# A message-passing kernel: GpSimd's gathers in the order in which they are written, with other waits

## The chip, the core and the metric

The kernel runs on one core of one Trainium2 chip. The metric is the device time of one execution in microseconds (us). Engines are named as in the profile: PE (TensorE, its weight loads in a row of their own, PEld), DVE (VectorE), ACT (ScalarE), POOL (GpSimd), SP (SyncE, which only issues DMAs here). L281 is line 281 of the kernel.

## The reference

It is one layer of a graph network with 6250 nodes of 128 features, and 100,000 edges that are sorted by their destination.

```python
msg_in = concat([x[src], x[dst], edge_attr], axis=1)      # 100000 x (128 + 128 + 4)
h = silu(msg_in @ mW1 + mb1)
messages = h @ mW2 + mb2
aggregated = segment_sum(messages, dst, num_segments=6250)
u = silu(concat([x, aggregated], axis=1) @ uW1 + ub1)
y = layer_norm(x + u @ uW2 + ub2)                          # ln_g, ln_b
out = layernorm(x + y)
```

All of it is float32.

## The kernel before, in words

The edges are cut into 98 groups of 1024 edges (8 tiles of 128 edges; the last group has 6 tiles). The part of the first layer that belongs to the source node is computed once for each node: `tab_a` = x @ mW1[:128], and so is the part of the destination, `tab_b`. Both tables are written to DRAM. For each group the source part is then fetched row by row: `fetch(g)` starts 8 indirect DMAs on POOL, each of which gathers 128 rows of 128 floats into one eighth of a buffer `ga`. There are six such buffers, so group g + 6 takes over the buffer of group g. Groups 0 to 4 (`g < RAW`) gather rows of x itself, since the table isn't there yet; PE multiplies these by the weights later, which is why they are turned first (`turn_rows`, `turn_late`).

The tables are made in 7 parts of 8 node tiles (`for k, (i0, n) in enumerate(parts)`): PE transposes x (L343), ACT copies it (L344), PE multiplies (L386), ACT copies one half of the products (L388) for `tab_a` and DVE adds a bias to the other (L389) for `tab_b`, and SP starts the two writes (L392, L393). They use three tiles of psum in turn. Between these parts stand the lists of destinations (`destination_lists`, k = 2) and the turning of the groups 0 to 3 (L365 on PE, L366 on DVE).

The loop over groups then does at step g, for later groups as well:

- `load(g + 4)` on SP: 96 rows of `tab_b` into `mv`, edge attributes into `st`
- `hidden(g)`: DVE adds the gathered rows to the products (`s`, L635), ACT makes silu of it (`h`, L636); for g < 5 ACT alone
- `products(g + 2)`: 8 matmuls of PE (L619), for g < 5 with 8 more of the gathered rows (L622)
- `node_matrix(g + 3)` and `edge_matrix(g + 1)` on DVE: matrices of zeros and ones (L592, L605)
- `by_nodes(g)`: 8 matmuls of PE (L647) that sum the edges of a node; DVE adds the sums of group g - 2 to `acc` (L660)
- `fetch` of a group further on
- one step of a `node_batch`, the second layer for some 512 nodes (L510 to L560)

A matmul on float32 appears as two rows of PE and two of PEld in the profile, a transpose as one of each. At g = 4 `destination_checks` and at g = 5 `fuse_weights` are inserted, both with short exchanges between PE and DVE or ACT.

The order of the instructions of SP, PE, DVE and ACT is the order in which they are written (`manual_schedule`). POOL is not in that list: its instructions are ordered by the framework's scheduler. In the program as built, this scheduler issues of a group gathers 1, 2, 3, 5, 6, 7 ahead of those gathers which have a wait added by hand; in the steady part gather 0 of group g comes 8th, and gather 4 follows behind the first three of group g + 1.

Waits are added by hand in `fetch(g, *after)` with `add_manual_dep`: with two instructions in `after`, gather 0 waits for the first and gather 4 for the second. `begun[g]` is the first matmul of `products(g)`, `summing[g]` the first of `by_nodes(g)`. From group 14 on (`CLOSE`) group g + 2 is fetched at step g and waits for `begun[g + 2]` and `summing[g]`. Groups 8 to 13 are fetched at every second step, and wait for `begun` of two groups. Besides these, the first gather of a group that is issued waits until the buffer is free, and each gather waits for the landing of the eighth before it.

Of the kernel before, what the change touches and what calls it, by code (L numbers as in the profile page):

```python
# [14 lines left out]
ENG = mybir.EngineType  # L15
# [9 lines left out]
def kernel(  # L25
# [40 lines left out]
    nc = tc.nc  # L66
# [13 lines left out]
    CLOSE = 14  # L80
    LEAD = 4
    RAW = 5
# [14 lines left out]
    def groups(n, g):  # L97
        return [(i, min(g, n - i)) for i in range(0, n, g)]
# [12 lines left out]
    batches.append((NT - LAST, LAST, NG))  # L111

    edges = ExitStack()
    edges.enter_context(tc.manual_schedule(engines={ENG.SP, ENG.PE, ENG.DVE, ENG.Activation}))
    gath = edges.enter_context(tc.tile_pool(name="gath", bufs=6))
    work = edges.enter_context(tc.tile_pool(name="edge", bufs=2))

# [4 lines left out]
    def wide():  # L122
        return tables_ps.tile([P, G, P], F32, name="wide")
# [50 lines left out]
    ident = consts.tile([P, P], F32, name="ident")  # L174
# [48 lines left out]
    def destination_lists():  # L223
        base_c = work.tile([NG, 1], F32, name="base_c", bufs=1)
        nc.vector.tensor_copy(base_c, dst_l[:, 0:1])
        rel_n = work.tile([P, GE], F32, name="s")[:NG]
        nc.vector.tensor_scalar(rel_n, dst_l, base_c, None, op0=OP.subtract)

        near_n = work.tile([P, GE], F32, name="s")[:NG]
        nc.vector.tensor_scalar(near_n, rel_n, float(W), -1.0, op0=OP.min, op1=OP.max)  # L230
        near_u = tpool.tile([NG, GE], U8, name="near_u")
        nc.vector.tensor_scalar(near_u, near_n, 1.0, None, op0=OP.add)
        nc.sync.dma_start(near_d[:, :], near_u)
        by_lane(rel, rel_n)
        row = to_row(base_c, NG)
        nc.vector.tensor_copy(base_f, row)
        nc.vector.tensor_copy(base_i, row)
# [34 lines left out]
    rows, bases, near = {}, {}, {}  # L272

    def tiles_of(g):
        return min(G, -(-(E - g * GE) // P))

    def fetch(g, *after):

        rows[g] = gath.tile([P, G, H], F32, name="ga")
        for i in range(tiles_of(g)):  # L280
            ins = nc.gpsimd.indirect_dma_start(  # L281
                out=rows[g][:, i, :],
                out_offset=None,
                in_=x if g < RAW else tab_a[:, :],
                in_offset=bass.IndirectOffsetOnAxis(
                    ap=src_i[:, g, i : i + 1] if g else src_0[:, i : i + 1], axis=0
                ),
            )
            part, at = divmod(i * len(after), G)
            if after and at == 0:  # L290
                tc.add_manual_dep(
                    ins.ins,
                    after[part].ins.name,
                    mybir.DependencyInfo(
                        mybir.DependencyClass.Sync, mybir.DependencyReason.DATA
                    ),
                    reason="TensorE keeps up with the gathers",
                )
# [8 lines left out]
    def attributes(c):  # L307
        t = turn.tile([EQ, EJ * ED], F32, name="ea_l")
        chunk = edge_attr[c * EC : (c + 1) * EC]
        nc.sync.dma_start(t, chunk.rearrange("(q j) d -> q (j d)", q=EQ))  # L310
        ea_l[c] = t
# [21 lines left out]
    def by_node(t):  # L333
        return t[:NP].rearrange("(i p) f -> p i f", p=P)
# [5 lines left out]
    def turn_x(i0, n):  # L340
        pt = wide()
        for i in range(n):
            ins = nc.tensor.transpose(pt[:, i, :], x_sb[:, i0 + i, :], ident)  # L343
        nc.scalar.copy(xT[:, i0 * P : (i0 + n) * P], pt[:, :n, :].rearrange("p i f -> p (i f)"))  # L344
        return ins
# [12 lines left out]
    parts = groups(NT, G)  # L358
    table = []

    def turn_rows(g):

        px = wide()
        for i in range(G):
            nc.tensor.transpose(px[:, i, :], rows[g][:, i, :], ident)  # L365
        nc.vector.tensor_copy(rows[g], px)  # L366

    def turn_late(g):
        for lo in range(0, G, BT):
            px = node_y()  # L370
            for i in range(BT):
                nc.tensor.transpose(px[:, i, :], rows[g][:, lo + i, :], ident)
            nc.vector.tensor_copy(rows[g][:, lo : lo + BT], px)

    fetch(1, turn_x(*parts[0]))
    for k, (i0, n) in enumerate(parts):
        if k + 1 < len(parts):
            turn_x(*parts[k + 1])

        tb = x_sb[:, i0 : i0 + n, :]  # L380
        ta = tpool.tile([P, G, H], F32, name="t", bufs=2)
        for j0, m in groups(n, G // 2):
            pm = wide().rearrange("p (i s) f -> p i s f", s=2)
            for j in range(m):
                cols = slice((i0 + j0 + j) * P, (i0 + j0 + j + 1) * P)
                ins = nc.tensor.matmul(pm[:, j], xT[:, cols], w1, start=True, stop=True)  # L386
            own = slice(j0, j0 + m)
            nc.scalar.copy(ta[:, own], pm[:, :m, 0, :])  # L388
            nc.vector.tensor_add(  # L389
                tb[:, own], pm[:, :m, 1, :], b1[:, None, :].to_broadcast([P, m, H])  # L390
            )
        nc.sync.dma_start(by_node(tab_a)[:, i0 : i0 + n, :], ta[:, :n])  # L392
        nc.sync.dma_start(by_node(tab_b)[:, i0 : i0 + n, :], tb)  # L393
        table.append(ins)
        if k == 0:
            attributes(0)
        if k == 1:
            fetch(2, *table)
            for t in mv:
                nc.sync.dma_start(t[W:], mW1[2 * H :])  # L400
        if k == 2:
            destination_lists()
        if k == 3:
            fetch(3, *table[2:])
            attribute_rows(0)
            turn_rows(0)
        cols = slice(i0 * P, NW if i0 + n == NT else (i0 + n) * P)
        nc.vector.memset(acc[:, cols], 0.0)
        if k == 4:
            fetch(4, table[4])  # L410
            destinations(0)
            load_bases(0)
            turn_rows(1)
    for g in range(2, TURNED):
        turn_rows(g)
    if E < NG * GE:
        pad = tpool.tile([ED, NG * GE - E], F32, name="pad")
        nc.vector.memset(pad, 0.0)
# [5 lines left out]
    def rows_ps():  # L424
        return ps.tile([P, G, P], F32, name="pre")

    def node_y():
        return node_ps.tile([P, BT, H], F32, name="y")
# [181 lines left out]
        )  # L610
        return oh

    begun, summing = {}, {}

    def products(g):
        pre = rows_ps()
        st = stbuf[g % NST].rearrange("k (i c) -> k i c", i=G)
        for i in range(tiles_of(g)):
            ins = nc.tensor.matmul(pre[:, i, :], st[:, i, :], mv[g % NM], start=True, stop=g >= RAW)  # L619
            begun.setdefault(g, ins)  # L620
            if g < RAW:
                nc.tensor.matmul(  # L622
                    pre[:, i, :], rows[g][:, i, :], w1[:, 0, :], start=False, stop=True
                )
        return pre

    def hidden(g):
# [24 lines left out]
    def by_nodes(g, h, oh):  # L652

        pt = degrees(g)
        sums(g, pt, h, oh, 0, tiles_of(g))
        return pt
# [14 lines left out]
    oh, h, pt, running = {0: edge_matrix(0)}, {}, {}, []  # L671
    pre = {g: products(g) for g in range(2)}

    for g in range(RAW, 8):
        fetch(g)
    for g in range(NG):
        if g == 3:
            load_weights()
        if g == 4:
            destination_checks(node_y())  # L680
        if g == 5:
            fuse_weights()
        for c in range(1, NC):
            if g == max(1, c * EC // GE - 10):
                attributes(c)
            if g == max(1, c * EC // GE - 10) + 1:
                attribute_rows(c)
        if g + LEAD < NG:
            load(g + LEAD)
        last = g >= NG - 1  # L690
        if not last:
            h[g] = hidden(g)
        if TURNED <= g + 2 < RAW:
            turn_late(g + 2)
        if g + 2 < NG:
            pre[g + 2] = products(g + 2)
        if g + MADE < NG:
            node_matrix(g + MADE)
        if g + 1 < NG:
            oh[g + 1] = edge_matrix(g + 1)  # L700
        if g - 2 in pt:
            add(g - 2, pt.pop(g - 2))
        if last:
            break
        pt[g] = by_nodes(g, h.pop(g), oh.pop(g))
        if CLOSE <= g + 2 < NG:
            fetch(g + 2, begun[g + 2], summing[g])
        elif g % 2:
            at = g // 2 + 8
            fetch(at, begun[g + 1], begun[g + 2])  # L710
        if g >= NG - 3:
            add(g - 1, pt.pop(g - 1))
        for i0, n, first in batches[:-1]:
            if g == (first if first >= NG - 3 else first + 1):
                running.append(node_batch(i0, n, *node_tiles(nodes, node_y)))
        for _ in range(2 if g >= NG - 6 else 1):
            advance(running)

    g = NG - 1
# [194 lines left out]
```

## Time and profile before

| | us |
|---|---|
| median of 3 runs (1204.91 to 1206.64) | 1206.59 |
| the profiled execution, its own time | 1194.18 |
| its span, first to last instruction | 1192.3 |
| POOL busy, 790 instructions | 740.9 |
| PE busy, 3655 rows | 723.3 |
| DVE busy | 488.3 |
| ACT busy | 244.9 |

The mean granted clock of PE was 0.685 of full speed. The span is that of one profiled execution, and the durations of single instructions come from it. A row of POOL named DMA_INDIRECT is one gather of 128 rows. The bracket behind a row of the timeline is the time for which the engine had been idle, and what ended it; "issue" means that the profile shows no wait, and "remote" that the one who ended it is not known to it.

### The profile page before, as it was taken

What the parts mean: (1) busy time and instruction counts of PE and PEld (TensorE: products, weight loads), DVE (VectorE), ACT (ScalarE), POOL (GpSimd) and SP (SyncE); (2) the same over time, 40 slices, a digit from 0 to 9 for tenths busy, and PEclk for the clock granted to TensorE, in tenths of its full rate; (3) what the DMA queues carried; (4) which work ended last, traced back from release to release, by engine and by line L of the source; (5) the groups of instructions that cost most, each with busy time, mean ns of one, the idle gap of its engine ahead of it and who ended that gap; (6) DMA issues with size and microseconds to landing.
All of it is one profiled execution on the core that took longest, in us unless ns stands there. A gap on an engine that the chain in (4) does not pass through costs nothing.

```text
span 1192.3 us, 11417 instructions
## 1 busy us (share of the span) xinstructions
PE 723.3 (61%) x3655; PEld 646.4 (54%) x3655; DVE 488.3 (41%) x1023; ACT 244.9 (21%) x306; POOL 740.9 (62%) x790
## 2 busy tenths in 40 slices
PE   3765388655755664575466466566556575565664
PEld 3655378545655654465465456456556464555553
DVE  3460366352443343334335325225326335236253
ACT  1221024112112222212122103102202202112233
POOL 7536456766666666566566666666666666666650
PEclk9787667766765676667667667666676666676765
DMA  7653123223222222232222223213322222222210
GB/s 187 177 164 89 37 60 83 71 53 79 77 64 66 79 69 65 54 91 60 76 71 64 73 52 85 73 49 78 83 51 79 79 52 75 74 53 64 57 48 24
DMA packets 70222, 88.96 MB, mean 75 GB/s; under 512 B 20720, under 2 KB 51839, under 8 KB 70155
## 3 DMA queue, kind: packets, MB, share of 16 engines
q0 software_dynamic: 25024, 51.30, 17.5%
q1 hardware_dynamic: 40552, 34.96, 9.9%
q10 hardware_dynamic: 4578, 1.89, 0.7%
q8 instruction: 31, 0.51, 0.2%
q14 instruction: 37, 0.30, 0.1%
HBM read 76.71 MB, written 11.38 MB: 74 GB/s over the span
## 4 chain that ended last, share of the span: by engine, by line
issue 39%; POOL 25%; PE 16%; another core or an unknown queue 6%; DVE 5%; DMA 1%; DVEq 1%; ACT 1%; SPq 0%; POOLq 0%; ACTq 0%
POOL ga L281 25%; PE pre L619 7%; PE pt L647 6%; DVEq L635 1%; DVE oh L605 1%; DMA ga<-tab_a,src_i 1%; DVE s L635 1%; DVE st L484 1%; PE y L526 1%; DVE y L528 1%; PE y L517 0%; PE y L510 0%; PE y L511 0%; PE y L512 0%
## 5 line engine op out<-in xcount | busy, mean ns | idle before, releaser
L281 POOL DMA_INDIRECT ga<-tab_a,src_i x742 | 701.8, 946 | 393.7 <-issue 194.4
L619 PE MATMUL pre<-mv,st 100*128 100x128 f32 x1564 | 315.7, 364 | 195.8 <-issue 141.7
L647 PE MATMUL pt<-oh,h 128*128 128x96 f32 x1564 | 292.2, 341 | 188.5 <-issue 177.5
L619 PEld LDWEIGHTS pre<-mv,st 100*128 100x128 f32 x1564 | 286.3, 271 | 215.6 <-issue 168.1
L647 PEld LDWEIGHTS pt<-oh,h 128*128 128x128 f32 x1564 | 276.1, 259 | 205.9 <-issue 196.8
L635 DVE TENSOR_TENSOR s<-ga,pre 128x1024 f32<-128x1024 f32 x92 | 112.2, 1220 | 435.4 <-DMA ga<-tab_a,src_i 213.1
L636 ACT ACTIVATE h<-s 128x1024 f32<-128x1024 f32 x92 | 97.1, 1056 | 656.0 <-issue 336.0
L592 DVE TENSOR_SCALAR_CACHE_REDUCE st<-near,p_next 96x1024 f32<-96x1024 uint8 x98 | 124.2, 1269 | 3.6 <-DMA ea_d<-pad 2.0
L605 DVE TENSOR_TENSOR oh<-w_row,rel 128x768 f32<-128x768 f32 x98 | 93.1, 950 | 19.8 <-remote 16.8
L528 DVE TENSOR_TENSOR y<-y,xs 128x512 f32<-128x512 f32 (+2 forms) x13 | 8.4, 648 | 116.0 <-issue 103.3
L281 POOL DMA_INDIRECT ga<-in_x_dram,src_i x32 | 30.3, 947 | 20.0 <-issue 8.2
L636 ACT ACT_TABLE_LOAD x25 | 32.1, 1283 | 19.8 <-remote 17.9
L386 PE MATMUL wide<-w,xT 128*128 128x256 f32 x98 | 27.9, 441 | 12.6 <-issue 9.2
L526 PEld LDWEIGHTS y<-u,uT 128*128 128x128 f32 x94 | 23.1, 322 | 20.9 <-issue 20.8
L490 ACT ACT_TABLE_LOAD x26 | 33.4, 1283 | 3.5 <-DVE mv L485 3.1
L526 PE MATMUL y<-u,uT 128*128 128x128 f32 x94 | 26.7, 422 | 7.8 <-issue 7.7
L386 PEld LDWEIGHTS wide<-w,xT 128*128 128x128 f32 x98 | 21.0, 223 | 18.1 <-issue 9.7
L515 ACT ACTIVATE uT<-y,ub_col 128x512 f32<-128x512 f32 (+2 forms) x13 | 8.4, 645 | 103.7 <-remote 78.6
L665 DVE TENSOR_TENSOR deg<-deg,pt 1x96 f32 x98 | 24.4, 249 | 1.0
L660 DVE TENSOR_TENSOR acc<-acc,pt 128x96 f32 x98 | 23.7, 242 | 1.8 <-PE pt L647 1.7
L485 DVE BATCH_NORM_AGGREGATE mv<-st 128x2 f32<-128x6 f32 x98 | 17.8, 182 | 15.5 <-remote 5.2
L622 PE MATMUL pre<-w,ga 128*128 128x128 f32 x80 | 20.2, 339 | 3.9 <-issue 3.9
(122 smaller groups left out, 372.0 us busy)
## 6 DMA issues: line engine op xcount, KB each, us to landing
ga<-tab_a,src_i POOLq DMA_INDIRECT x742
near<-near_d SPq DMA_DIRECT2D x24, 384.0 KB
mv<-tab_b SPq DMA_DIRECT2D x98, 48.0 KB
tab_a<-t SPq DMA_DIRECT2D x6, 512.0 KB
tab_b<-x_sb SPq DMA_DIRECT2D x6, 512.0 KB
xs<-in_x_dram SPq DMA_DIRECT2D x11, 256.0 KB
out_dram<-z SPq DMA_DIRECT2D x11, 256.0 KB
st<-ea_d SPq DMA_DIRECT2D x98, 16.0 KB
```

The lines of the kernel that those rows point to most:

```text
L281: ins = nc.gpsimd.indirect_dma_start(out=rows[g][:, i, :], out_offset=None, in_=x if g < RAW else tab_a[:, :], in_offset=bass.IndirectOffs ...
L386: ins = nc.tensor.matmul(pm[:, j], xT[:, cols], w1, start=True, stop=True)
L490: nc.scalar.activation(r[:, :n], mv[:, :n, 1], AF.Sqrt, bias=eps)
L526: nc.tensor.matmul(y[:, i, :], by_p[:, :, i], u2, start=False, stop=i == n - 1)
L592: nc.vector.tensor_scalar(stbuf[g % NST][:W], near.pop(g), p_next, 0.0, op0=OP.is_equal, op1=OP.add, accum_out=deg_q[g // DQ % 2][:, g % D ...
L605: nc.vector.tensor_tensor(oh, w_row[:, None, :].to_broadcast([P, G, W]), rel[:, g, :, None].to_broadcast([P, G, W]), op=OP.is_equal,)
L619: ins = nc.tensor.matmul(pre[:, i, :], st[:, i, :], mv[g % NM], start=True, stop=g >= RAW)
L635: nc.vector.tensor_add(s[:, :n], ga[:, :n], ps[:, :n])
L636: nc.scalar.activation(h[:, :n], s[:, :n], AF.Silu)
L647: ins = nc.tensor.matmul(pt[:, :W], h[:, i, :], oh[:, i, :], start=i == 0, stop=i == tiles_of(g) - 1)
L660: nc.vector.tensor_add(at, at, pt[:, :W])
L665: nc.vector.tensor_add(at, at, pt[row, W:])
```

## The change

POOL joins the engines whose instructions stand in written order. With this the added waits stand where they are written: at gather 0 and at gather 4. In the tables the waits of groups 1, 2, 3 and 4 are reduced to two, `table[0]` ahead of group 2 and `table[3]` in the middle of group 3 (`table[k]` is the last matmul of part k), and group 5 gets one in its middle for the last transpose of `turn_rows(3)`. A new dictionary `ended[g]` holds the last matmul of `products(g)`, and groups 6 to 13 wait for it, for `begun` or for `summing`, half by half. An entry of None in `after` is no wait.

```diff
-    edges.enter_context(tc.manual_schedule(engines={ENG.SP, ENG.PE, ENG.DVE, ENG.Activation}))
+    edges.enter_context(tc.manual_schedule(engines={ENG.SP, ENG.PE, ENG.DVE, ENG.Activation, ENG.Pool}))
...
             part, at = divmod(i * len(after), G)
-            if after and at == 0:
+            if after and at == 0 and after[part]:
...
-    fetch(1, turn_x(*parts[0]))
+    turn_x(*parts[0])
+    fetch(1)
...
         if k == 1:
-            fetch(2, *table)
+            fetch(2, table[0])
...
         if k == 3:
-            fetch(3, *table[2:])
+            fetch(3, None, table[3])
...
         if k == 4:
-            fetch(4, table[4])
+            fetch(4)
...
     for g in range(2, TURNED):
-        turn_rows(g)
+        ins = turn_rows(g)
+    fetch(RAW, None, ins)
...
             if g < RAW:
-                nc.tensor.matmul(
+                ins = nc.tensor.matmul(
                     pre[:, i, :], rows[g][:, i, :], w1[:, 0, :], start=False, stop=True
                 )
+            ended[g] = ins
...
-    for g in range(RAW, 8):
-        fetch(g)
+    fetch(6, None, ended[0])
...
         if CLOSE <= g + 2 < NG:
             fetch(g + 2, begun[g + 2], summing[g])
+        elif g == 0:
+            fetch(7, ended[1], begun[2])
+        elif g == 1:
+            fetch(8, begun[3], summing[1])
         elif g % 2:
-            at = g // 2 + 8
-            fetch(at, begun[g + 1], begun[g + 2])
+            fetch(g // 2 + 8, ended[g + 1], begun[g + 2] if g == CLOSE - 3 else ended[g + 2])
```

`turn_rows` now also returns its last transpose. The waits of groups 14 to 97 are written as before.

More of the change, by code (lines that the diff above doesn't have):

```diff
@@ L364, in turn_rows @@
         for i in range(G):
-            nc.tensor.transpose(px[:, i, :], rows[g][:, i, :], ident)
+            ins = nc.tensor.transpose(px[:, i, :], rows[g][:, i, :], ident)
         nc.vector.tensor_copy(rows[g], px)
+        return ins
     def turn_late(g):
@@ L611, in edge_matrix @@
         return oh
-    begun, summing = {}, {}
+    begun, ended, summing = {}, {}, {}
     def products(g):
```

## The prediction

> **What bounds the kernel now.** I read the page first (chain, then groups), then POOL's waits, then POOL's timeline from end to end, then the other engines around each gap.
>
> ```profile
> issue 39%; POOL 25%; PE 16%; another core or an unknown queue 6%; DVE 5%; DMA 1%; DVEq 1%; ACT 1%; SPq 0%; POOLq 0%; ACTq 0%
> ...
> L281 POOL DMA_INDIRECT ga<-tab_a,src_i x742 | 701.8, 946 | 393.7 <-issue 194.4
> ```
>
> The chain names POOL and "issue", the 0.30 us between two gathers. One gather is 0.944 us busy and 0.303 us to the next, a period of 1.247 us; all 782 take 975 of 1192.3 us. No other engine is so full (PE 723), so the span is a ledger of POOL's gaps. Gather 0 starts at 3.05 and gather 781 at 1157.84: 1154.8 minus 781 x 1.247 = 180.9 us of extra gaps. Cut at gather 40 (74.81, the first from `tab_a`) and at gather 112 (195.18), they are 21.9 us in the **tables**, 30.6 us in the **ramp** of groups 5 to 13, and 128.4 us in the **steady** part. Behind the last gather lies a fixed tail of 34.5 us.
>
> POOL's waits and two gaps of its timeline, with PE's rows before the second:
>
> ```profile
> POOL ga L281 <- remote: 132.1, 48, 4.0
> ...
> 499.80 0.94 POOL L281 DMA_INDIRECT ga<-tab_a,src_i  x1 [0.30 <-issue]
> 504.07 0.94 POOL L281 DMA_INDIRECT ga<-tab_a,src_i  x1 [3.33 <-remote]
> ...
> 521.02 0.37 PE L619 MATMUL pre<-mv,st 100*128 100x128 f32 x1 [1.72 <-issue]
> 527.04 0.94 POOL L281 DMA_INDIRECT ga<-tab_a,src_i  x1 [3.29 <-PE pre L619]
> ```
>
> The gap grows with the gathers since the gap before it, not with PE's work: after 8 gathers 1.94 to 2.26 us, after 12 some 2.7, after 16 3.3, after 20 3.97. I fit gap = 0.85 + 0.155n, which is 0.55 us per pause and 0.155 us per gather above the usual 0.30. Check on the steady part: 669 x 0.155 + 46 pauses x 0.55 = 129.0, found 128.4. So the 0.155 us must be paid whatever the order is; only the number of pauses and true waiting can change.
>
> What ends such a pause is seen best where one engine has nothing else to do:
>
> ```profile
> 114.73 0.60 PE L372 MATMUL y<-ident,ga 128*128 128x128 f32 x4
> ...
> 125.58 0.94 POOL L281 DMA_INDIRECT ga<-tab_a,src_i  x1 [0.31 <-issue]
> 129.29 0.69 DVE L373 COPY ga<-y 128x512 f32<-128x512 f32 x1 [44.42 <-remote]
> ...
> 131.85 0.94 POOL L281 DMA_INDIRECT ga<-tab_a,src_i  x1 [5.33 <-PE pre L619]
> ```
>
> DVE needs only the four transposes that end at 115.33, yet starts at 129.29, 2.8 us after POOL fell silent (126.52). PE's news is **held back while POOL issues without a pause**, and let go when POOL has paused for about the gap above. Counting PE's rows (weight loads and matmuls) since the previous restart: news of rows up to 64 or 66 passes (`ended[3]`, ACT's copy at 55.83, a later `summing`), news of rows 76, 82, 83 and 116 is held. After some 110 to 150 rows PE itself drops to one row per 0.6 to 0.7 us. The same is seen in the tables:
>
> ```profile
> 15.70 4.38 PE L386 MATMUL wide<-w,xT 128*128 128x256 f32 x16
> ...
> 28.41 0.58 ACT L388 COPY t<-wide 128x512 f32<-128x512 f32 x1 [9.54 <-remote]
> 34.04 0.59 ACT L388 COPY t<-wide 128x512 f32<-128x512 f32 x1 [5.04 <-PE wide L386]
> ...
> 34.28 0.94 POOL L281 DMA_INDIRECT ga<-in_x_dram,src_i  x1 [3.74 <-PE wide L386]
> ...
> 74.81 0.94 POOL L281 DMA_INDIRECT ga<-tab_a,src_i  x1 [11.47 <-DMA tab_a<-t]
> ```
>
> PE's 16 products end at 20.08; ACT copies the second half at 34.04, as POOL's 3.74 us pause ends.
>
> [...]
>
> **The change, part by part.** *Order.* The program as built before issues a group's gathers 1, 2, 3, 5, 6, 7 first and the two with a manual wait later: in the steady part gather 0 (waits `begun[g]`) as the 8th and gather 4 (waits `summing[g-2]`) three to four into the next group. In written order they stand 1st and 5th, 6 gathers (7.5 us) earlier in POOL's stream for the same event of PE. Nothing is computed more or less; SP's, ACT's and DVE's queues keep their order, and no DMA is added. POOL's initial constants end at 1.53 us either way, 1.5 us before the first list lands: no cost.
>
> *Tables.* After: 16 gathers, wait `table[0]`, 12 gathers, wait `table[3]`, 12 gathers, then `tab_a`. The first pause comes at 23.05 instead of 30.54 and ends near 26.4 (gap for 16: 3.3), so ACT's second copy is at about 26.6, 7.4 us sooner. That shrinks: `k = 1` is 4 us sooner, `k = 2` (needs the pause at 41.3, over at 44.0) 1.6 us. From there POOL is silent and PE, ACT and DVE run as before from 46.3 to 55.03 (8.7 us): `table[3]` at about 53.5. Then come 12 gathers, 53.8 to 68.8, where before only two were left. PE's rows behind `table[3]`: transposes of group 0 16, of x 16, `k = 4` 32, together 64, so that table gets through; transposes of group 1 are rows 65 to 80 and are held, DVE's copy with them, and with it the psum tile that the second half of `k = 5` needs. It goes on when news trickles out or POOL has paused, 68 to 71.4. From DVE's copy to the first `tab_a` gather took 8.7 us before (66.09 to 74.81): 77 to 80. I take 78, **+3 us**; below stands 70.5 (before's 19.8 us from `table[3]` less its own 2.9 of holding), above 80.
>
> *Ramp*, from the first `tab_a` gather = 0. Groups 5 to 7 run as before: pause at 9.7, 16 gathers, pause at 31.4 to 34.9. Before, group 8 and six of group 9 followed without need of PE; after, half 8b asks `summing[1]` (PE 38.2, passes), and 9a asks `ended[4]`. PE waits there for DVE's L373, held at row 76. POOL now stops at 44.9; DVE goes on at 46.6 instead of 54.5; from L373 to the end of the products took 6.5 us (129.29 to 135.8): 9a starts at 53.4. Before, 7 gathers more were out, at 61.3; less 7 x 1.247 that is 52.5. Then 9b at 58.4 to 59.9 (`ended[5]`, row 64), 10a at 66 to 70 (`ended[6]` stands behind the ping-pong of `destination_checks`, 2.7 us from 146.10 to 148.82, and DVE's 3.4 us of L253 to L263), 10b at 77.5 to 81 (`ended[7]` behind sums, `fuse_weights` and products, 9.2 us in the trace). The remaining 28 gathers cost 35 + 4.3 + 5 pauses x 0.55 = 42: 119.5 to 123, middle 121.5, against 120.4. **+1 us**, from -8 (only pauses, no waiting for PE: 112) to +4. What gains here, DVE 8 us sooner, is spent on waiting for `ended[6]` and `ended[7]`, while POOL stands still.
>
> *Steady.* Waits come every 4 gathers and 32 rows of PE. At a restart PE is some 46 rows past the event asked for (before: all 32 of `begun[48]`'s products and 14 of the next), so three waits pass and the fourth, 128 rows on, is held: 16 gathers. After, gather g is complete 4 gathers (5 us) later relative to `begun[g+2]`, so PE's lead shrinks to about 30; the third wait, 96 rows on, is then at the limit of 96 and half of the cycles break at 12 gathers. 669/13 = 51 pauses instead of 46: 5 x 0.55 = **+3 us**; from -3 (40 pauses) to +21 (84, every 8 gathers). The tail keeps its 34.5 us.
>
> Sum: +3 +1 +3 = +7 on a profiled execution of 1194.18 us (span 1192.3 and 1.9 around it). The median of the three runs, 1206.59, is 12.4 above it; I add the 7 there: **1214**.
>
> **Rivals.** *Faster*: the limit is not one of rows but of time since a restart (held news is mostly over 8 us old). Then group 1's copy is let through, `tab_a` is ready at 70.5 (-4.3) and the ramp pays pauses alone, 112 (-8.4): about **1194**. It decides at one point: whether DVE's copy of group 1 starts within 2 us of PE's transposes. For it: nothing in the tables has a gap near 5 us any more, and the pauses of the ramp are short. Against it: ACT's copy of 28.41 was held while only 64 rows were out. *Pause at every group*: PE's lead in the steady part falls below 5 rows and each `begun[g]` is held; 84 pauses, +21 +4: **1232**. For it: 2.2 us gaps after 8 gathers at 180.80 and 192.68; against: they are rare from 204 on. *Nothing to see*: the new waits are passed as before and the shifts cancel, **1207**; a wait already met costs nothing in the trace (133 of the 190 gathers that wait for PE start within 0.5 us).
>
> **Numbers.** Forecast 0.50, pause at every group 0.13, both slower; no change 0.12; faster 0.25. What a measurement can tell from no change is about 0.2%, 2.4 us. The range takes in the faster case and the pause at every group: 1194 to 1232.
>
> **What would show it.** Right: a first gap before gather 16, a second before gather 28; first `tab_a` gather at 77 to 80 and DVE's L366 copy held some 8 us; L373 at about 46 to 47 us behind that gather; gaps only at multiples of 4 gathers, some 50 behind gather 112, of 2.7 and 3.3 us. Wrong: `tab_a` gathers by 72, or fewer than 44 steady gaps, or gaps that no longer follow 0.85 + 0.155n.

## The result, and the profile after

| | before | after |
|---|---|---|
| median, 12 executions each (us) | 1206.91 | 1205.34 |
| lowest to highest | 1204.91 to 1211.60 | 1201.51 to 1207.88 |
| profiled execution, own time | 1194.18 | 1207.88 |
| its span | 1192.3 | 1206.1 |
| mean granted clock of PE | 0.685 | 0.654 |

The ratio of the times is 0.9985, with a 95% interval of 0.9970 to 0.9999: 1.6 us faster, at the edge of what this measurement can tell, as the interval only just leaves out 1. The forecast was 1214 and slower.

Profile against profile, after is 13.8 us *slower*. Its pauses stand where the forecast put them, though the stages between them differ in size. The contradiction of times and profiles is what the experiments are about. First the steps. Page of after, the chain by engine and the costliest group (busy and mean ns, then idle time before it):

```profile
PE 33%; issue 33%; POOL 15%; DVE 7%; another core or an unknown queue 7%; DMA 2%; ACT 1%; SPq 0%; ACTq 0%; DVEq 0%; POOLq 0%
...
L281 POOL DMA_INDIRECT ga<-tab_a,src_i x742 | 703.1, 948 | 406.2 <-issue 201.5
```

The gathers cost what they cost before (701.8 us busy then); the idle time before them has grown from 393.7 to 406.2 us. Timelines of after, tables and ramp, POOL, ACT, DVE and POOL again (start, duration, then in the bracket the idle time and what ended it):

```profile
25.93 0.94 POOL L281 DMA_INDIRECT ga<-in_x_dram,src_i  x1 [2.91 <-remote]
53.03 0.95 POOL L281 DMA_INDIRECT ga<-in_x_dram,src_i  x1 [12.39 <-PE wide L365]
78.62 0.94 POOL L281 DMA_INDIRECT ga<-tab_a,src_i  x1 [10.88 <-DMA tab_a<-t]
...
24.92 0.59 ACT L390 COPY t<-wide 128x512 f32<-128x512 f32 x1 [7.22 <-remote]
...
125.20 0.69 DVE L374 COPY ga<-y 128x512 f32<-128x512 f32 x1 [36.23 <-remote]
...
133.07 0.95 POOL L281 DMA_INDIRECT ga<-tab_a,src_i  x1 [9.69 <-PE pre L625]
```

The pauses stand ahead of gathers 16 and 28, as forecast; the first gather from `tab_a` is at 78.62 (forecast 77 to 80, taken 78); DVE's L374 (L373 before) comes 46.6 us behind it (forecast 46 to 47). Behind gather 112 there are 48 pauses (forecast 51), all at multiples of 4 gathers, of 2.68 us on average after 12 gathers and 3.47 after 16. Against before, the tables are 3.8 us longer (forecast 3), the ramp 6.1 (forecast 1), the steady part 8.3 (forecast 3), and the tail is 4.6 shorter (forecast 0).

Cut into the four stages, us. Each column is one profile; the chip's number stands where it is known. A pause is here an idle time of over 0.8 us ahead of a gather:

| | before, on record | after, on record | before, chip 15 | after, chip 14 | before, chip 7 | after, chip 7 | order alone, chip 7 |
|---|---|---|---|---|---|---|---|
| gather 40 starts (tables) | 74.8 | 78.6 | 58.8 | 58.1 | 80.5 | 76.9 | 71.2 |
| gathers 40 to 112 (ramp) | 120.4 | 126.5 | 89.9 | 89.9 | 120.1 | 120.1 | 115.1 |
| gathers 112 to 781 (steady) | 962.7 | 971.0 | 838.4 | 837.2 | 962.1 | 961.7 | 961.4 |
| behind the start of gather 781 (tail) | 34.5 | 29.9 | 32.0 | 28.9 | 35.0 | 29.2 | 30.8 |
| pauses in the steady part | 46 | 48 | 0 | 0 | 46 | 50 | 45 |

### The profile page after: what moved, and what is told of

The parts are those of the page before. It is cut to its first block, busy times and chain, and to the rows that moved or that the text cites. A ratio compares the mean times of both kernels' runs of the same rounds, so it can differ in the third digit from the quotient of the medians.

```text
span 1206.1 us, 11356 instructions
## 1 busy us (share of the span) xinstructions
PE 762.4 (63%) x3655; PEld 682.4 (57%) x3655; DVE 488.4 (40%) x1023; ACT 245.3 (20%) x306; POOL 742.2 (62%) x790
## 4 chain that ended last, share of the span: by engine, by line
PE 33%; issue 33%; POOL 15%; DVE 7%; another core or an unknown queue 7%; DMA 2%; ACT 1%; SPq 0%; ACTq 0%; DVEq 0%; POOLq 0%
POOL ga L281 15%; PE pre L622 14%; PE pt L651 12%; PE y L529 2%; DVE oh L608 1%; DMA ga<-tab_a,src_i 1%; DVE st L595 1%; PE wide L388 1%; PE y L520 1%; DVE st L487 1%; PE y L513 1%; DVE s L639 1%; PE y L514 1%; DVE deg L669 1%
## 5 line engine op out<-in xcount | busy, mean ns | idle before, releaser
L281 POOL DMA_INDIRECT ga<-tab_a,src_i x742 | 703.1, 948 | 406.2 <-issue 201.5
L622 PE MATMUL pre<-mv,st 100*128 100x128 f32 x1564 | 342.5, 394 | 243.0 <-issue 202.6
L622 PEld LDWEIGHTS pre<-mv,st 100*128 100x128 f32 x1564 | 312.6, 298 | 264.8 <-issue 227.4
L651 PEld LDWEIGHTS pt<-oh,h 128*128 128x128 f32 x1564 | 280.0, 266 | 146.1 <-issue 140.7
L281 POOL DMA_INDIRECT ga<-in_x_dram,src_i x32 | 30.3, 946 | 24.4 <-PE wide L365 12.4
L640 ACT ACT_TABLE_LOAD x25 | 32.1, 1283 | 22.5 <-remote 17.6
```

Of the source, the lines that this page charges most:

```text
L281: ins = nc.gpsimd.indirect_dma_start(out=rows[g][:, i, :], out_offset=None, in_=x if g < RAW else tab_a[:, :], in_offset=bass.IndirectOffs ...
L640: nc.scalar.activation(h[:, :n], s[:, :n], AF.Silu)
L651: ins = nc.tensor.matmul(pt[:, :W], h[:, i, :], oh[:, i, :], start=i == 0, stop=i == tiles_of(g) - 1)
```

## Experiments

Times are against the kernel before on the same chip, taken beside them. The number of the chip tells which may be compared with which.

**The kernel before again, and three parts of the change (chip 15).** `order_alone` is before with one edit:

```diff
-    ...engines={ENG.SP, ENG.PE, ENG.DVE, ENG.Activation}))
+    ...engines={ENG.SP, ENG.PE, ENG.DVE, ENG.Activation, ENG.Pool}))
```

`order_tables` is after with before's waits for groups 6 to 13, `order_ramp` is after with before's waits for groups 1 to 5.

> The kernel before, unchanged, to see whether its profiled execution (1194.18 us, span 1192.3, PE clock 0.685), to which the forecast's +7 was added, stands for its usual execution (1206.9). Theory A, the profiled execution was an unusually short one: a second profile has a span of 1203 to 1208 at a clock below 0.67; gather 40 stays at 75 within 2 us and the 12 us lie between gather 40 and gather 781 (gather 112 later than 195.2, or more than 46 pauses after it). Theory B, the written change really costs 13.8 us in a profiled execution and something else gives it back in the others: the second profile is at 1190 to 1196 again. Time against before: 1.000 in both.

> Only POOL in the list of engines in written order; all waits as before. Forecast's view: steady part +3 us (51 pauses instead of 46), the tables within 4 us of before (pauses at gathers 16, 20, 24, 28 and 32), so 1.000 to 1.006 of before. Rival, the order alone makes the loss and the new waits give it back: 1.008 or more. Rival, the order is worth nothing: within 0.998 to 1.002, the same number of steady pauses in both.

> Written order and the new waits of groups 0 to 5, but groups 6 to 13 wait as before (none for 6 and 7, begun of two groups from 8 on). Forecast's view: the first gather from tab_a at 77 to 80 as after (78.6), and the ramp 0 to 2 us shorter than after's 126.5 us from there to gather 112, since PE's news is asked for less often. Rival, the new waits of the ramp are what keeps news flowing: without them the ramp takes 130 us or more, and the time is 1.003 or more of before.

> Written order and the new waits of groups 6 to 13, but groups 1 to 4 wait as before and group 5 for nothing but its buffer and table. Forecast's view: the first gather from tab_a at 74 to 77, 3 us sooner than after, and the rest as after, so 3 us below after. Rival, five waits in written order stop POOL so often that the tables end later than with two: tab_a at 82 or more, and the time is 1.003 or more of before.

Neither theory had this: the same kernel before took 1022.98 us (the runs of before beside it: 1021.94, ratio 1.0004, 0.9995 to 1.0012). Its profile, page and waits of POOL (total, times, longest), then ACT in the tables and the copy of group 4:

```profile
L281 POOL DMA_INDIRECT ga<-tab_a,src_i x742 | 703.4, 948 | 231.7 <-issue 187.8
...
POOL ga L281 <- PE pre L619: 7.3, 24, 0.3
...
20.13 0.59 ACT L388 COPY t<-wide 128x512 f32<-128x512 f32 x1 [1.78 <-PE wide L386]
21.86 0.59 ACT L388 COPY t<-wide 128x512 f32<-128x512 f32 x1 [1.14 <-PE wide L386]
...
82.02 0.60 PE L372 MATMUL y<-ident,ga 128*128 128x128 f32 x4
...
82.66 0.69 DVE L373 COPY ga<-y 128x512 f32<-128x512 f32 x1 [13.78 <-PE y L372]
```

A gather is as long as ever (948 ns with its outliers, median 944), but the idle time before gathers has gone from 393.7 to 231.7 us: no wait for `pre` is longer than the usual 0.3 us. ACT copies the two halves at 20.13 and 21.86, not at 28.41 and 34.04. DVE starts its L373 at 82.66, 0.04 us behind the end of PE's transposes (82.02 + 0.60), where the profile of record had it 14 us behind. **I see no news held on this chip, and there is no pause behind gather 112**: 669 gathers take 838.4 us, 1.253 each.

There all three parts are faster than before by the same: `order_alone` 1016.65 (0.9943, 0.9930 to 0.9956), `order_tables` 1015.84 (0.9938, 0.9926 to 0.9951), `order_ramp` 1015.47 (0.9936, 0.9923 to 0.9948). All show a tail of 29.0 us where before has 32.0. So on this chip the written order alone gives the gain, and what the two sets of new waits add to it is within the 1.2 us between the three. What was expected of single stages isn't tested by it, since no pause is there to move.

**The kernels again, and two tests of the pauses (chip 14).** `even_waits` and `more_rows` change after by

```diff
-            fetch(g + 2, begun[g + 2], summing[g])
+            if g % 2:
+                fetch(g + 2)
+            else:
+                fetch(g + 2, begun[g + 2], None)
```
```diff
             begun.setdefault(g, ins)
+            if g >= RAW and i % 2:
+                nc.tensor.matmul(pre[:, i, :], st[:, i, :], mv[g % NM], start=True, stop=True)
```

> The kernel before once more. Theory C, formed on the last runs: the pauses and the held news belong to the chip or its state on which a run falls, not to the kernel. Then this profile is of one of two kinds, with nothing between: span 1019 with no pause behind gather 112, gather 40 at 59 and gather 112 at 149; or span 1192 to 1206 with 46 or more pauses, gather 40 at 75 and gather 112 at 195 or later. Rival: pauses come and go within one chip, and the count lies anywhere from 0 to 60.

> The kernel after, unchanged. On a chip without pauses, theory C expects the sum of what is left there: tables -2, ramp 0, steady -1.6, tail -3.1 (the tail that order_alone, order_tables and order_ramp all showed, 29.0 against 32.0), together 1015 to 1016 or 0.993 to 0.995 of before. On a chip with pauses: 0.997 to 1.000 as measured, and gather 112 some 6 to 10 us later than before, the steady part as before within 3 us, the tail 4.5 us shorter. Rival: the waits of the ramp cost something even without pauses, 0.996 or more there.

> The kernel after, but from group 14 on only the even groups wait, and only at gather 0 (begun). By the price of 0.55 us for each pause: on a chip with pauses they come each 16 gathers, 42 instead of 48 after gather 112, so 3 us below after. Rival, fewer pauses hold news longer and PE, at one row in 0.65 us once it is held, falls behind: 48 pauses or more in length, 10 us above after. On a chip without pauses both expect after's time within 0.5 us.

> The kernel after, but four of the eight matmuls of products are done twice from group 5 on, which adds 16 rows to the 64 of a group (the result is the same). Limit counted in rows: on a chip with pauses no cycle of 16 gathers is left behind gather 112, most have 8 or 12, 60 to 84 pauses instead of 48, 7 to 20 us above after. Limit by time since the restart: 48 pauses within 4, and 0 to 3 us above after. On a chip without pauses, POOL sets the pace in both: after's time within 2 us.

Chip 14 has no pauses behind gather 112 either. Before took 1024.31 once (span 1022.4), the runs of before beside it 1022.79; its four stages are 58.0, 93.0, 839.2 and 32.2 us, with a single wait of 3.4 us ahead of gather 48. After took 1016.16: **0.9935 (0.9921 to 0.9948)**, as theory C of `before_look` expected, with gather 40 at 58.1 and a tail of 28.9. `even_waits` 1016.48 (0.9936, 0.9923 to 0.9950) and `more_rows` 1017.44 (0.9944, 0.9930 to 0.9957) are within 1.3 us of after: a quarter more rows of PE brings no pause here. On the price of a pause the two say nothing.

**Tail and waits (chip 4, which has pauses: before 1194.52).** `tail_only` is before, where groups 96 and 97 are fetched without added waits; `no_waits` is after without any of them; `more_records` is `more_rows` with 24 copies of one element on ACT and 24 on DVE in each group.

> The kernel before, with the scheduler's order, but groups 96 and 97 are fetched without added waits, so that their 14 gathers alone stand in written order. Theory: the shorter tail comes from group 96 being complete 6 gathers before the last one instead of 3. Then the tail is 29.0 us as in order_alone, not 32.1, at unchanged first stages, and that is half of the gain: -3 us, 0.996 to 0.998 of before. Rival: the tail is shorter because PE is further along when all groups stand in written order; then nothing changes here, tail 31.5 to 32.5 and 0.999 to 1.001.

> The kernel after without any of the added waits, in written order; each gather still waits for its buffer, its list or table, and the landing of the eighth before it. On a chip without pauses, theory: the added waits cost and bring nothing there, so after's time within 1.5 us (0.992 to 0.995 of before). Rival: they keep POOL from delaying others even there, 1.000 or more of before. On a chip with pauses: no pause but those for buffers, news held for up to six groups, PE at one row in 0.65 us, and 1.02 or more of before.

> The kernel after with more instructions in each group: four of the products' matmuls done twice (16 rows of PE), 24 copies of one element on ACT and 24 on DVE, into tiles that nothing reads. About 155 rows in a group instead of 90. Theory R, [...] with 1.7 times the records pauses appear behind gather 112 on the chip where there were none, 5 or more. Theory S, the pauses are a property of the chip or of its state that the rate of records does not touch: no pause behind gather 112, and POOL's period stays at 1.249 us; the span within 8 us of 1014.

`no_waits` took 1326.88 us, **1.110 (1.1059 to 1.1141)**. Its waits of POOL and one stretch of PE:

```profile
POOL ga L281 <- DVE s L639: 233.5, 32, 14.0
...
621.48 0.37 PE L622 MATMUL pre<-mv,st 100*128 100x128 f32 x1 [0.60 <-issue]
622.88 0.79 PE L622 MATMUL pre<-mv,st 100*128 100x128 f32 x2 [1.03 <-issue]
624.28 0.37 PE L622 MATMUL pre<-mv,st 100*128 100x128 f32 x1 [0.60 <-issue]
```

With nothing to stop POOL, it runs on for 16 or 24 gathers until a buffer is missing, while PE is let through one matmul at a time; then it stands for 7 to 8 us. So on this chip the added waits pay for themselves by making POOL pause early. The same kernel was not run on a chip without pauses.

`tail_only` was a badly made test. It took 1203.24 us (1.0069, 1.0047 to 1.0091), slower, with a tail of 48.3 us: without waits no pause came behind gather 758, and PE had single matmuls behind 1.1 to 2.5 us of idle time from 1149 to 1158. It says nothing of the position.

`more_records` took 1217.83 us once, with 76 pauses: 39 after 8 gathers, 24 after 12, 12 after 4 and only one after 16, where after has 23 to 25 after 16. POOL's timeline:

```profile
503.85 0.95 POOL L281 DMA_INDIRECT ga<-tab_a,src_i  x1 [1.06 <-PE pre L624]
515.75 0.94 POOL L281 DMA_INDIRECT ga<-tab_a,src_i  x1 [2.20 <-remote]
527.61 0.94 POOL L281 DMA_INDIRECT ga<-tab_a,src_i  x1 [2.16 <-remote]
545.23 0.95 POOL L281 DMA_INDIRECT ga<-tab_a,src_i  x1 [2.73 <-PE pt L659]
```

POOL stops some 10 us after a restart instead of 15 to 20. That could also mean that PE, with more to do, is itself late. What tells the two apart is when PE had ended the matmul that a pausing gather asks for. In after on chip 7 it had ended 5.2 to 13.0 us before POOL went on, and before POOL fell silent, in all 50 pauses of the steady part: the news was held. In `more_records` the same is so for 68 of the 76, among them all 39 after 8 gathers (3.4 to 10.2 us); in the other 8 PE ended it only after POOL had fallen silent.

With a limit by time since the restart, the matmuls held should end as late after it as before. They ended 5.3 us (median) behind POOL's last restart in `more_records`, but 9.3 in after on record and 11.1 on chip 7. Counted in rows of PE, PEld, DVE and ACT since that restart it is 86 against 83 and 83. So **a number of instructions fits better than a time**; it is no sharp limit, as waits passed in `more_records` with up to 9.2 us and 101 rows. Whether PE's rows alone count or those of ACT and DVE too, this one profile can't settle, as it adds both. Nor did the run test what was expected of it on a chip without pauses. The law of the gaps holds: 1.74, 2.09, 2.73 and 3.39 us after 4, 8, 12 and 16 gathers (law 1.47, 2.09, 2.71 and 3.33), and 669 x 0.155 + 76 x 0.55 = 145.5 us of extra gaps in the steady part, found 152.5 (986.8 less 669 x 1.247).

**A pair from one chip with pauses (chip 7, before 1194.35).** `tail_late` is after, but gather 4 of group 96 is issued as the fourth last of all:

```diff
...
+        order = [(g, i) for i in range(tiles_of(g))]
+        if g == NG - 2:
+            order.remove((g, 4))
+            moved[0] = after[1]
+        if g == NG - 1:
+            order.insert(3, (g - 1, 4))
+        for q, i in order:
...
```

> The kernel before, for a profile from the same chip as the next three. On a chip with pauses: gather 40 at 74 to 76, gather 112 at 193 to 196, 44 to 48 pauses behind it, tail 34 to 35; a chip on which before takes 1207 instead of 1194 shows its 12 us in longer pauses (3.5 us instead of 3.3 after 16 gathers) and a longer ramp, not in more of them. Rival: the 12 us are more pauses, 58 or more.

> The kernel after, on that chip. If the 13.8 us between the profiled executions belong to the chips: 0.995 to 1.002 of before, the tables +3 to +4, the ramp +2 to +6, the steady part within 5 us of before's on the same chip, the tail -4 to -5. If they belong to the change: 1.008 or more, with the steady part 8 us longer. On a chip without pauses 0.9935 again.

> Only the written order, on that chip. With pauses, forecast's view: the tables as before within 4 us, the ramp with 8 pauses for begun of two groups that are met late, so 121 to 128 us, the steady part and the tail as after_again_2: within 0.5% of after. Rival, the new waits of tables and ramp carry the result: order alone 1.01 or more of before. Without pauses 0.994 again.

> The kernel after, but gather 4 of group 96 is issued as the fourth last of all gathers, where it stood before the change, not as the tenth last; its wait is met by then. If group 96 being complete sooner makes the shorter tail: tail +3.0 to +4.5 us against after on the same chip (32 us without pauses, 33 to 35 with), and the time as much longer. Rival, PE's lead over POOL makes it: the tail as after within 1 us.

After took 1191.11 us, **0.9967 (0.9952 to 0.9982)**, 3.2 us below before; its profile has a span of 1187.9, against 1206.1 of the same kernel on record. **The 13.8 us between the profiles on record are therefore no effect of the change**: the same kernel after lost 18.1 us from one profile to the other (tables 1.8, ramp 6.4, steady 9.3). Before has 1194.35 here and 1194.52 on chip 4, where the profiled 1194.18 would be an ordinary execution; none of the 12 timed runs on record came below 1204.91. So that profile probably came from another chip than the times beside it; the records don't name it. The rise of 12 us that I expected to see in longer pauses wasn't met on chip 7, so where it lies for before stays open; for after it is in the ramp and in pauses of 3.47 instead of 3.11 us after 16 gathers. The granted clock does not explain it: after had 0.654 on record and 0.666 here, and the order alone, the fastest on this chip, has 0.662.

The order alone took **1180.24 us, 0.9875 (0.9851 to 0.9898)**: the best of all, 14.1 us below before and 10.9 below after. My expectation of it (within 0.5% of after, ramp 121 to 128) was wrong. POOL's pauses in the tables and ACT's copy of the first half of part 5, first of the order alone, then of after on the same chip:

```profile
33.84 0.94 POOL L281 DMA_INDIRECT ga<-in_x_dram,src_i  x1 [3.28 <-PE wide L386]
47.27 0.94 POOL L281 DMA_INDIRECT ga<-in_x_dram,src_i  x1 [3.46 <-PE wide L365]
...
62.91 0.58 ACT L388 COPY t<-wide 128x512 f32<-128x512 f32 x1 [6.80 <-PE wide L386]
...
71.17 0.94 POOL L281 DMA_INDIRECT ga<-tab_a,src_i  x1 [9.02 <-DMA tab_a<-t]
```
```profile
53.00 0.94 POOL L281 DMA_INDIRECT ga<-in_x_dram,src_i  x1 [12.37 <-PE wide L365]
...
68.64 0.59 ACT L390 COPY t<-wide 128x512 f32<-128x512 f32 x1 [6.78 <-PE wide L388]
...
76.87 0.94 POOL L281 DMA_INDIRECT ga<-tab_a,src_i  x1 [9.16 <-DMA tab_a<-t]
```

Both pause ahead of gather 16. Before's five waits, in written order, pause again ahead of gather 20, so PE's news goes out at 30.6 to 33.8; after has no wait there, runs 12 gathers to 40.6 and then stands 12.4 us, since PE has been held and `table[3]` is far off. The pause that the change took out was useful: 5.7 us in the tables. Both kernels then have 12 gathers to go. In both PE has ended the products of that first half (at 59.38 and at 64.45), but ACT copies them only 0.8 and 0.9 us behind the end of POOL's last gather before `tab_a` (62.15 and 67.71), and the first `tab_a` gather follows 8.3 and 8.2 us later. Up to there the two kernels differ in nothing but the waits of groups 1 to 5. The ramp is 5.0 us longer than with the order alone: 10a starts 66.9 us behind the first `tab_a` gather with `ended[6]` asked for, 62.4 with `begun[6]`. That `ended` causes all of it is my reading of the stages; the test of it did not reach a chip with pauses (below).

`tail_late` took 1193.98 us (0.9981, 0.9963 to 0.9998), 2.9 above after, with a tail of 32.1 instead of 29.2, also 2.9. **The place of this one gather therefore makes a part of the shorter tail**, but 2.9 is the most that it can be given, because the profiles also differ in where POOL pauses last:

```profile
1153.77 0.94 POOL L281 DMA_INDIRECT ga<-tab_a,src_i  x1 [3.37 <-remote]
```
```profile
1157.44 0.94 POOL L281 DMA_INDIRECT ga<-tab_a,src_i  x1 [1.84 <-remote]
```
```profile
1140.64 0.94 POOL L289 DMA_INDIRECT ga<-tab_a,src_i  x1 [3.41 <-remote]
```

These are gather 774 of before, 780 of after and 768 of `tail_late`, all on chip 7. The order alone, whose last gathers stand as in after, also pauses last ahead of gather 768: its tail of 30.8 is 1.3 below that of `tail_late`. Without pauses the written order as a whole shortens the tail by 3.1 us on chip 15 (32.0 to 29.0) and by 3.3 on chip 14 (32.2 to 28.9).

ACT's silu of group 96 and POOL's last gather, before and after on record:

```profile
1161.89 1.06 ACT L636 ACTIVATE h<-s 128x1024 f32<-128x1024 f32 x1
...
1157.84 0.95 POOL L281 DMA_INDIRECT ga<-tab_a,src_i  x1 [0.30 <-issue]
```
```profile
1173.98 1.06 ACT L640 ACTIVATE h<-s 128x1024 f32<-128x1024 f32 x1
...
1176.12 0.95 POOL L281 DMA_INDIRECT ga<-tab_a,src_i  x1 [0.30 <-issue]
```

Before, the silu of group 96 stands 4.1 us behind the last gather; after, 2.1 us ahead of it. Gather 4 of group 96 was the fourth last; now the group is complete 6 gathers before the last one.

**Three more, meant for a chip with pauses.** `order_ramp_2` is `order_ramp` again; `after_begun` and `order_best` are

```diff
-            fetch(g // 2 + 8, ended[g + 1], begun[g + 2] if g == CLOSE - 3 else ended[g + 2])
+            fetch(g // 2 + 8, begun[g + 1], begun[g + 2])
```
```diff
+        if k == 5:
+            fetch(4, table[4], mid)
         if k == 4:
-            fetch(4, table[4])
...
```

the latter on the order alone, with the waits of `even_waits`; `mid` is the last product of the first half of part 5.

> Written order with the new waits of groups 6 to 13 and the old ones of groups 1 to 4. On a chip with pauses: if the two losses are separate, gather 40 at 71 to 72 as in order_alone_2 (71.2) and the ramp 119 to 121 us as after's (120.1), so 1185 where before is 1194, 0.990 to 0.994. If the longer ramp is a consequence of the tables' end: ramp 115 to 116 and 0.986 to 0.989. Without pauses: 0.9935 as before.

> The kernel after, but groups 9 to 13 wait for begun of two groups, as before the change, where it has ended; one line. On a chip with pauses: if asking for the last product in place of the first makes the longer ramp, it falls from 120.1 to 115 to 116.5 us at unchanged tables (76 to 78.6), and the time by 4 to 5 us, 0.991 to 0.995 of before. If the pauses' number makes it (order_alone_2 has 11 in the ramp, after 9), nothing within 1.5 us. Without pauses: 0.9935.

> Only the written order and the old waits, with two edits: the second half of group 4 waits for the last product of the first half of part 5 (a pause near 57 us, where POOL has 9 us to spare before tab_a is ready), and from group 14 on only the even groups wait, at gather 0. On a chip with pauses: gather 40 at 69 instead of 71.2 (2 us), 42 pauses behind gather 112 instead of 45 (1.6 us), so 1176 to 1178 where before is 1194, 0.984 to 0.987. Rival: the pause near 57 delays the gathers of group 4 past the table, 0.988 or more. Without pauses 0.992 to 0.995.

They fell on chip 14, without pauses: 1016.63 (0.9950, 0.9936 to 0.9964), 1017.21 (0.9945, 0.9932 to 0.9958) and 1017.15 (0.9947, 0.9934 to 0.9959), as all others in written order there. What they were to tell apart stays open.

## Why the prediction was wrong

The forecast added +7 us to a median; the change gave -1.6 on the chip of record and -3.2 on chip 7. By its steps, on chip 7, where both kernels have a profile:

- **Tail, the step that failed.** "The tail keeps its 34.5 us" put at nothing a term that the order moves: it is 29.2, from 35.0, so -5.8 (on record 29.9, so -4.6). The argument was at hand: the steady step says that a group's gathers change their place relative to PE's events, but I carried that into PE's lead alone and not to the last two groups. 3 gathers x 1.247 = 3.7 us was to be had from the order, and the chips without pauses show 3.1 and 3.3 of it. How much of that is the place of gather 4 of group 96 is known only as 1.3 to 2.9 (`tail_late`); gather 0 of group 97, second last before, now comes ahead of the group's others as well. The rest of the 5.8 shows only with pauses: before's tail is 3.0 us longer on chip 7 than on chip 15, after's 0.4 longer than on chip 14. It goes with the last pause, 7 gathers before the last one in before and one before it in after; no run tests that.
- **Steady, the right count at a wrong price.** 50 pauses instead of 46 (forecast 51), yet -0.4 us instead of +3. After 12 gathers a pause was 2.47 us and after 16 3.11, below the 2.7 and 3.3 of the law, which makes up for the four more. Why they were shorter there is open: with the same waits in the steady part, `tail_late` and the order alone have 3.29 and 3.30 after 16.
- **Tables, right in number for after, wrong for before.** Gather 40 came at 78.6 and 76.9 (taken: 78), but in part by luck. The forecast has DVE's copy of group 1 (L366) held until 68 to 71.4, and 8.7 us from there. On record it started at 63.81, and 14.8 us were left: PE's products waited for ACT's copy at 65.91. On chip 7 both were over by 62.0 while POOL was still issuing, and the products of part 5 were held in their place until POOL had stopped, as shown above. And before isn't fixed at 74.8: three profiles of its tables on chips with pauses have 74.55, 74.81 and 80.52. In the third POOL stands 0.97 us ahead of gather 8, and its first long pause comes ahead of gather 29 instead of 22; that the one leads to the other isn't shown. So the +3 was measured from a single draw; against 80.5 it is -3.6.
- **Ramp, right on chip 7.** +0.0 (120.07 to 120.10; taken +1), and halves 10a and 10b start 66.9 and 78.7 us behind the first `tab_a` gather (forecast 66 to 70 and 77.5 to 81). On record they start at 72.9 and 84.6, and the ramp is +6.1: the same kernel's two profiles differ by 6.4.

Sum on chip 7: -3.6 + 0.0 - 0.4 - 5.8 = -9.8, the difference of the two spans (1197.7 and 1187.9). Before's profiled execution there took 1199.5, against a median of 1194.35. With 74.8 in its tables the sum would be -4.1, near the measured -3.2.

Of the rivals, "nothing to see" came nearest with its 1207, and half its reason is right: the shifts cancel, though not because waits are passed as before. "Faster" (`tab_a` at 70.5, no holding) fell in the tables of after:

```profile
57.80 1.04 PE L365 MATMUL wide<-ident,ga 128*128 128x128 f32 x8
58.67 0.27 PE L343 MATMUL wide<-ident,x_sb 128*128 128x128 f32 x1
...
63.81 1.23 DVE L366 COPY ga<-wide 128x1024 f32<-128x1024 f32 x1 [2.65 <-remote]
...
65.91 0.27 ACT L344 COPY xT<-wide 128x128 f32<-128x128 f32 x1 [6.55 <-remote]
```

DVE's L366 starts 5.0 us behind PE's transposes (forecast some 8), though from 59.41 to 62.46 of it DVE's queue has a register load of L348, which isn't counted as busy. ACT's L344, which had nothing else to do, starts 7.0 us behind its own. On chip 7 the same two are 3.2 us (0.5 behind the end of the load) and 2.7 us. "Pause at every group" fell with the counts.

Deeper lies a sentence in which I took a trace for the kernel: "the 0.155 us must be paid whatever the order is". On chips 14 and 15 nobody pays it: the same program has no pause behind gather 112 (669 gathers in 838.4 and 839.2 us) and takes 1022 us. No run shows what sets these chips apart from 4 and 7.

**Open:** what makes a chip pause, and whether it would pause if nothing were recorded (each execution here has a span and a clock on record); whether the losses of the new waits in tables and ramp are separate, and whether `ended` makes the second; what the last pause adds to the tail; where before loses 12 us from chip 7 to the chip of record.

## What to carry to other kernels

Never subtract two profiles before you know that they come from one chip: here one kernel's span varied from 1014 to 1206 us, against an effect of 3. Where an engine's order changes, look also at the end of the program: what is fetched last has a part in the tail. And test the smallest part of a change by itself: one word in a list of engines gave 14 us on a chip with pauses, of which the waits added with it took back 11.

## What the runs showed of the hardware

- The same program ran at 1022 us on chips 14 and 15 and at 1194 on chips 4 and 7, a ratio of 1.17. The gathers did not make it: 742 of them took 948 ns on average in before on chip 15, and 946 in before on record, which has pauses.
- In the profile from chip 15 DVE's L373 starts 0.04 us behind the end of PE's transposes, as far as the profile gives that end; in before on record it starts 14 us behind it, 2.8 us after POOL has fallen silent. On chip 7 all 50 steady pauses of after were for matmuls that PE had ended 5 to 13 us earlier. A pause of POOL is not always needed: in after on record DVE's L366 started at 63.81 and ACT's L344 at 65.91, while POOL was issuing until 67.73.
- On chip 4, which holds news, the kernel without the added waits took 1.110 of before's time: 30 pauses of 7 to 8 us on average behind gather 112, where profiles of before show some 46 of mostly 2 to 4 us.
